# Expert tiles transposed by VectorE in 32x32 blocks instead of TensorE, with loads ahead and on two queues

## Chip, cores and metric

The kernel runs on one core of a Trainium2 chip. The metric is device time in microseconds (us). The kernel before takes 638.38 us, the median of 3 runs (637.48 to 639.96).

## What is computed

The reference is one block of a transformer: gated linear cross-attention with 16 heads of 32, then a mixture of 8 experts of which each token takes 2. There are 4 batches of 512 tokens, 1024 context rows each, and width 512, all in float32. Cut to what matters:

```python
x = x + xattn(layernorm(x), ctx, Wq, Wg, bg, Wkv, Wo)
xn = layernorm(x)
w, sel = top_k(xn @ Wr, 2)               # two experts for each token
gate = one_hot(sel) weighted by softmax(w)
for e in range(8):
    out = out + gate[..., e] * (xn @ We[e] + be[e])
x = x + out
```

## The kernel before

**Attention.** For each batch the kernel makes keys and values of the context in eight tiles, sums them to a small matrix per head, projects queries and gates, and adds the output projection to `x`. TensorE's instructions are kept in the order in which the program writes them (`matmul` at L85, `transpose` at L88). The other engines' instructions are ordered by a scheduler when the program is built, unless an edge or a `keep_in_program_order` pins them; each engine and each DMA queue then works in that fixed order and waits on semaphores.

**Routing.** `choose` normalizes a batch's tokens, makes the router's logits and takes the two largest. `dispatch` counts tokens per expert and lets GpSimd scatter each token's normalized row, with two numbers behind it (where the result goes, and the first choice), into `stream`, a DRAM buffer with one region for each expert. A row there has ROW = 514 elements, 2,056 bytes.

**Expert tiles.** `listed` makes, on the chip, a list of tiles of 128 consecutive stream rows: for each, the row at which it starts and its expert. `run` works through a list. In `rows(j)` SyncE reads the start from the list into a register (L624) and loads the 128 rows (L632) into `xg`, which lies in one of five buffers (three with tag `cT`, two with tag `v`). Four TensorE transposes (`transposed`, L220) turn `xg` into PSUM, and ScalarE copies the result to `xgT` (tag `qT`, four buffers, which the attention's queries use as well). `expert(j)` multiplies with the expert's weights in eight TensorE instructions, VectorE adds the bias into `y` (L659, three buffers), and GpSimd computes each row's home (`at`, L665) and scatters `y` to `result` in DRAM (L670).

There are two lists. The early one has 17 tiles (EARLY) that are full of tokens of the first three batches; four of them run ahead of the last batch's output projection, the others among its routing. The late one is made after the last `dispatch`; 18 tiles (SURE) always run, and up to four more stand in two nested branches (L835), which were not taken here. Before the late list, tiles of `empty` rows are written behind each expert's last token (fills, L775). Rows of the late list wait for all writes to the stream.

**The end.** `fetch(q)` loads the results of two output tiles back in two DMAs of 512 KB, `add(t)` adds both choices to `x` with two VectorE operations (L803), `store(t)` writes an output tile from ScalarE's queue. `at_step` says after which late tile each of these stands. The first eight output tiles' results are complete after the late tile of index DONE_2 - 1 (8 tiles), the next four's after DONE_3 (14 tiles), and the last four's after all.

**The inputs' loads.** SyncE's queue issues all loads, in program order where `load` (L92) is used, among them the experts' weights (one DMA of 1 MB per expert, during the second and third batch's attention).

Of the kernel before, what the change touches and what calls it, by code (L numbers as in the profile page):

```python
# [1 line left out]

# [7 lines left out]
F32 = mybir.dt.float32  # L10
# [5 lines left out]
ET = mybir.EngineType  # L16

P = 128
B, L, S, D = 4, 512, 1024, 512
E, F = 8, 512  # L20
HD = 32
NC = D // P
# [26 lines left out]
def xattn_moe_kernel(  # L49
# [39 lines left out]
        tc.keep_in_program_order(nc.tensor.transpose(dst, src, ident))  # L89


    def load(dst, src):  # L92
        tc.keep_in_program_order(nc.sync.dma_start(out=dst, in_=src))

    def load_ctx(b, s):
        t = cpool.tile([P, ROW], F32, tag="cT", name=f"cT_{b}_{s}")
# [15 lines left out]
    wo_sb = wpool.tile([P, NC, D], F32, tag="wo", name="wo_sb")  # L112
    wr_sb = wpool.tile([P, NC, E], F32, name="wr_sb")
    bg_sb = wpool.tile([P, NC], F32, name="bg_sb")
    we_sb = wpool.tile([P, E, NC, F], F32, name="we_sb")

    ctx_tiles = {}
    ctx_tiles[0, 0] = load_ctx(0, 0)
# [162 lines left out]
    def kv_tiles(b, lo, hi, between=None):  # L281
        for s in range(lo, hi):
            nxt = (b, s + 2) if s + 2 < NS else (b + 1, s + 2 - NS)
            if nxt[0] < B and nxt != (0, 2):
                ctx_tiles[nxt] = load_ctx(*nxt)
            if b in (1, 2) and s % 2 == 0:
                e = (b - 1) * E // 2 + s // 2
                load(we_sb[:, e], we[e])
            if (b, s) == (3, 0):
                load(stream[SLOTS : SLOTS + P, :], empty)  # L290
            if s == 0:
                sums[b] = pkv.tile([P, NC, 2 * P], F32, tag="kvs", name="kvs")
            k = made.pop(s) if s in made else keys(b, s)
            if (b, s) == (0, 0):
                made[1] = keys(0, 1)
            v = values(b, s)
            if s > 0:
                kv_add(sums[b], s - 1, *pending[b])
            pending[b] = k, v
            if between is not None:  # L300
                between(s - lo)
        if hi == NS:
            kv_add(sums[b], NS - 1, *pending[b])
# [314 lines left out]
    def run(lists, lo, n, early):  # L618
        why = "clamped to the tiles of the streams and to the experts where it is computed"
        no_i, row_i, ranked = lists  # L620

        def rows(j):

            row = nc.values_load(  # L624
                row_i[0:1, j : j + 1], [ET.SP], min_val=0, max_val=SLOTS,
                skip_runtime_bounds_check_because=why,
            )
            if j % 5 < 3:
                xg = cpool.tile([P, ROW], F32, tag="cT", name="xg")
            else:  # L630
                xg = kvpool.tile([P, ROW], F32, tag="v", name="xg", bufs=2)
            load = nc.sync.dma_start(out=xg, in_=stream[ds(row, P), :])  # L632
            if early:
                behind(load, written["stream"][: 2 * NT * (B - 1)], "tokens of the tile")
                early_loads.append(load)
                for put in scatters.get(B - 1, []):
                    tc.declare_no_dep(load.ins, put.ins, reason=full_already)
            else:
                behind(load, written["stream"], "tokens of the tile")
            xT = work.tile([P, NC, P], F32, tag="qT", name="xgT", bufs=NC)  # L640
            transposed(xT, xg)
            return xT, xg

        def expert(j, xT, xg):
            no = nc.values_load(
                no_i[0:1, j : j + 1], [ET.PE, ET.DVE], min_val=0, max_val=E - 1,
                skip_runtime_bounds_check_because=why,
            )
            pe = pmm.tile([P, F], F32, tag="mm", name="pe")
            for c in range(NC):  # L650
                matmul(
                    out=pe,
                    lhsT=xT[:, c, :],
                    rhs=we_sb[:, ds(no, 1), c, :].rearrange("p o f -> p (o f)"),
                    start=(c == 0),
                    stop=(c == NC - 1),
                )
            y = kvpool.tile([P, F], F32, tag="k", name="y")
            nc.vector.tensor_tensor(  # L659
                y, pe, be_sb[:, ds(no, 1), :].rearrange("p o f -> p (o f)"), ALU.add  # L660
            )
            home_i = small.tile([P, 1], U32, tag="to", name="to", bufs=8)

            at = small.tile([P, 1], F32, tag="at", name="at", bufs=8)
            nc.gpsimd.tensor_scalar(  # L665
                at, xg[:, D + 1 : D + 2], ranked[:, j : j + 1], xg[:, D : D + 1],
                ALU.is_equal, ALU.add,
            )
            nc.gpsimd.tensor_scalar(home_i, at, unread[:, j : j + 1], None, ALU.min)
            put = nc.gpsimd.indirect_dma_start(  # L670
                out=result,
                out_offset=bass.IndirectOffsetOnAxis(ap=home_i, axis=0),
                in_=y,
                in_offset=None,
            )
            apart(put, "result", "each choice has a row; rows without a token go unread")
            for got in read_back:
                tc.declare_no_dep(put.ins, got.ins, reason="no token of these is in the tile")

        ready = rows(lo)  # L680
        for j in range(lo, n):
            cur, ready = ready, rows(j + 1) if j + 1 < n else None
            expert(j, *cur)
            yield


# [5 lines left out]
    for b in range(B):  # L692
# [10 lines left out]
        if not more:  # L703
            whole = per_expert("whole")
            nc.vector.tensor_scalar(whole, counts[b - 1], float(1 - P), None, ALU.add)
            full = tiles_of(whole, "full")
            held = [tiles_of(counts[1], "held2"), tiles_of(counts[2], "held3")]
            none = per_expert("none")
            nc.vector.memset(none, 0.0)
            ahead = per_expert("ahead")  # L710
            nc.vector.tensor_tensor(ahead, held[0], full, ALU.min)
            early_groups = spans([none, ahead, full], "A")
            early_list = listed(early_groups, EARLY, "A")
            be_sb = wpool.tile([P, E, F], F32, tag="wkv", name="be_sb")
            load(
                be_sb.rearrange("p e f -> p (e f)"),
                be.rearrange("(o e) f -> o (e f)", o=1).to_broadcast([P, E * F]),
            )
            early = run(early_list, 0, EARLY, True)
        products(qTs, z, aT)  # L720
        if more:
            xs[b + 1] = load_x(b + 1)
# [46 lines left out]
    nc.vector.tensor_tensor(ends, counts[B - 1], region[:, 0, :], ALU.add)  # L769
    for e in range(E):  # L770
        row = nc.values_load(
            ends[0:1, e : e + 1], [ET.SP], min_val=0, max_val=SLOTS - P,
            skip_runtime_bounds_check_because="a region has room for all tokens",
        )
        fill = nc.sync.dma_start(out=stream[ds(row, P), :], in_=empty)  # L775
        apart(fill, "stream", "rows behind the last token of a stream")
        for load in early_loads:
            tc.declare_no_dep(fill.ins, load.ins, reason="behind all tokens of the stream")
# [3 lines left out]
    homes = [(wpool, "wq"), (wpool, "wg"), (wpool, "wo"), (big, "xT"), (big, "aT")]  # L782
    fetched = {}

    def fetch(q, tiles):

        pool, tag = homes[q % len(homes)]
        yt = pool.tile([P, 2, 2, F], F32, tag=tag, name=f"y_{q}")
        for u in range(2):
            load = nc.sync.dma_start(out=yt[:, u], in_=flat[:, 2 * q + u])  # L790
            tc.keep_in_program_order(load)
            behind(load, written["result"][: EARLY + tiles], "results of the tokens")
            for put in written["result"][EARLY + tiles :]:
                tc.declare_no_dep(load.ins, put.ins, reason="no token of these is in the tile")
            read_back.append(load)
            fetched[2 * q + u] = yt[:, u]
# [16 lines left out]
    at_step = {}  # L813
    first, last = 2 * NT, (B - 1) * NT
    for q in range(first // 2):
        at_step.setdefault(DONE_2 + 2 + q, []).append((fetch, q, DONE_2))
    for q in range(first // 2, last // 2):
        at_step.setdefault(DONE_3 + 2, []).append((fetch, q, DONE_3))
    for t in range(last):
        step = min(DONE_2 + 3 + t, SURE - 1 - (last - 5 - t) // 2)  # L820
        at_step.setdefault(step, []).append((add, t))
        at_step.setdefault(max(step + 1, DONE_2 + 5), []).append((store, t))

    def also(j):
        for what, *of in at_step.pop(j, []):
            what(*of)

    for j, _ in enumerate(run(late_list, 0, SURE, False)):
        also(j)

    many = nc.values_load(
# [1 line left out]
        skip_runtime_bounds_check_because="the streams hold no more tiles",  # L833
    )
    with tc.If(many > SURE):  # L835
        for _ in run(late_list, SURE, SURE + 1, False):
            pass
        with tc.If(many > SURE + 1):
            for _ in run(late_list, SURE + 1, LATE, False):
                pass  # L840
    for j in sorted(at_step):
        also(j)
    for q in range(last // 2, TOK // P // 2):
        fetch(q, LATE)
    for t in range(last, TOK // P):
        add(t)
        store(t)
# [43 lines left out]
```

## Time and profile before

| what | value |
|---|---|
| median of 3 runs | 638.38 us |
| profiled execution: time | 640.01 us |
| profiled execution: span, first to last instruction | 638.3 us |
| mean granted TensorE clock | 0.984 |
| TensorE busy | 606.4 us, 95% of the span |
| VectorE, ScalarE, GpSimd busy | 37%, 21%, 17% |
| DMA traffic | 70.50 MB, mean 110 GB/s |
| expert tiles run | 17 early, 18 late |
| last product of an expert tile ends | 615.2 us |

A profile is one execution on the chip. PE is TensorE's matrix products and transposes, PEld its weight loads, DVE VectorE, ACT ScalarE, POOL GpSimd, SP SyncE; a q behind an engine's name means its instruction queue, which issues DMAs and waits. A group's line gives source line, engine, operation, out<-in, shape and count, then busy us, mean ns of one, and the idle time of the engine just before with what ended it. `pt` is the PSUM tile of a transpose, `pe` that of an expert tile's product, `pp` that of the counting matmuls in `dispatch`.

### The profile page before, as it was taken

The numbers are of one execution on the slowest core, as the hardware profiler recorded it, in microseconds if no ns is written. First come the engines' busy times: TensorE is split into PE (matmuls) and PEld (weight loads), VectorE is DVE, ScalarE is ACT, GpSimd is POOL, SyncE is SP. The second block draws the span as 40 slices with busy tenths as digits, with TensorE's granted clock in tenths as the row PEclk, the third lists the DMA queues.
The fourth block names the chain that finished last, engine by engine and source line by source line (L and its number), as shares of the span: only waits on it lengthen the run. The fifth ranks groups of instructions, "written<-read, shape, count | busy, mean of one in ns | idle before, by whom it ended". The sixth has DMA issues, their size and how long they took to land. (4 is left out here: it accounts for less than half of the span.)

```text
span 638.3 us, 6238 instructions
## 1 busy us (share of the span) xinstructions
PE 606.4 (95%) x2044; PEld 301.6 (47%) x2044; DVE 236.1 (37%) x562; ACT 135.5 (21%) x215; POOL 109.0 (17%) x244
## 2 busy tenths in 40 slices
PE   7999999999999999999999999999999999999950
PEld 3555543544564345455543544654444654444420
DVE  2222243126224521632534135148424272111583
ACT  1322222113322122042221113322111221111100
POOL 3100000000004000000230000005241354643420
PEclk9999999999999999999999999999999999999985
DMA  8611400220253023022130100033430269647768
GB/s 301 194 34 37 144 0 2 104 93 17 82 166 115 18 62 111 26 91 93 47 117 17 34 16 16 1 131 134 116 116 33 84 203 264 193 133 258 278 236 300
DMA packets 27376, 70.50 MB, mean 110 GB/s; under 512 B 4240, under 2 KB 4240, under 8 KB 25936
## 3 DMA queue, kind: packets, MB, share of 16 engines
q1 hardware_dynamic: 19680, 48.31, 23.7%
q0 software_dynamic: 5360, 17.60, 7.6%
q10 hardware_dynamic: 2304, 4.20, 1.8%
q8 instruction: 17, 0.28, 0.2%
q14 instruction: 15, 0.12, 0.1%
HBM read 45.93 MB, written 24.16 MB: 110 GB/s over the span
## 5 line engine op out<-in xcount | busy, mean ns | idle before, releaser
L86 PE MATMUL pe<-we_sb,xgT 128*128 x280 | 125.9, 594 | 1.1 <-issue 0.6
L86 PE MATMUL pk<-wkv_sb,cT 128*128 128x512 f32 x256 | 118.6, 608 | 4.6 <-DMA wkv_sb<-in_wkv_dram 4.6
L86 PE MATMUL pv<-wkv_sb,cT 128*128 128x512 f32 x256 | 114.9, 592 | 0.0
L86 PEld LDWEIGHTS pv<-wkv_sb,cT 128*128 128x128 f32 x256 | 48.6, 190 | 61.2 <-issue 61.0
L200 DVE TENSOR_SCALAR ex<-pk 128x512 f32<-128x512 f32 x32 | 22.0, 689 | 148.0 <-PE pk L86 148.0
L86 PEld LDWEIGHTS pe<-we_sb,xgT 128*128 128x128 f32 x280 | 50.6, 190 | 53.0 <-issue 52.0
L86 PEld LDWEIGHTS pk<-wkv_sb,cT 128*128 128x128 f32 x256 | 47.7, 194 | 58.1 <-issue 54.3
L257 POOL MEMSET v<- 128x4 f32 x32 | 3.3, 106 | 347.1 <-PE kvs L86 284.1
L201 ACT ACTIVATE ex<-ex 128x512 f32<-128x512 f32 x48 | 30.2, 630 | 138.7 <-DVE ex L200 128.8
L86 PE MATMUL pg<-xT,wg_sb 128*128 128x512 f32 x128 | 56.7, 595 | 0.0
L86 PE MATMUL pq<-xT,wq_sb 128*128 128x512 f32 x128 | 56.6, 596 | 0.0
L659 DVE TENSOR_TENSOR y<-pe,be_sb 128x512 f32<-128x512 f32 x35 | 24.1, 690 | 87.4 <-PE pe L86 73.5
L86 PE MATMUL po<-wo_sb,aT 128*128 128x512 f32 x128 | 55.6, 592 | 0.0
L225 ACT COPY xgT<-pt 128x512 f32<-128x512 f32 x35 | 20.3, 587 | 121.9 <-PE pt L89 103.5
L670 POOL DMA_INDIRECT result<-y,to x35 | 37.5, 1071 | 39.0 <-DVE y L659 32.1
L505 POOL DMA_INDIRECT stream<-row,slot x32 | 32.1, 1003 | 49.6 <-DVE cmp L533 22.5
L86 PEld LDWEIGHTS kvs<-v,k 128*128 128x128 f32 x256 | 33.3, 191 | 13.4 <-issue 13.4
L86 PEld LDWEIGHTS pg<-xT,wg_sb 128*128 128x128 f32 x128 | 24.0, 190 | 32.1 <-issue 32.1
L86 PEld LDWEIGHTS po<-wo_sb,aT 128*128 128x128 f32 x128 | 24.1, 190 | 29.2 <-issue 28.9
L86 PEld LDWEIGHTS pq<-xT,wq_sb 128*128 128x128 f32 x128 | 23.8, 190 | 27.3 <-issue 27.3
L86 PE MATMUL kvs<-v,k 128*128 128x129 f32 x256 | 34.0, 275 | 0.0
L202 DVE SCALAR_TENSOR_TENSOR k<-pk,ex 128x512 f32<-128x512 f32 x32 | 22.1, 691 | 24.1 <-ACT ex L201 24.0
(151 smaller groups left out, 445.6 us busy)
## 6 DMA issues: line engine op xcount, KB each, us to landing
xg<-stream SPq DMA_DIRECT2D x35, 257.0 KB
cT<-in_cT_dram SPq DMA_DIRECT2D x32, 256.0 KB
we_sb<-in_we_dram SPq DMA_DIRECT2D x8, 1024.0 KB
y<-result SPq DMA_DIRECT2D x16, 512.0 KB
x<-in_x_dram SPq DMA_DIRECT2D x16, 256.0 KB
out_dram<-x ACTq DMA_DIRECT2D x16, 256.0 KB
stream<-empty SPq DMA_DIRECT2D x9, 257.0 KB
wkv_sb<-in_wkv_dram SPq DMA_DIRECT2D x8, 256.0 KB
```

Source lines behind the costliest of these rows:

```text
L86: tc.keep_in_program_order(nc.tensor.matmul(**operands))
L200: nc.vector.tensor_scalar(ex, src, 0.0, None, ALU.min)
L201: nc.scalar.activation(ex, ex, AF.Exp)
L202: nc.vector.scalar_tensor_tensor(dst, src, 0.0, ex, ALU.max, ALU.add)
L225: nc.scalar.copy(dst, pt)
L257: nc.gpsimd.memset(v[:, :, P : P + 1], 1.0)
L505: put = nc.gpsimd.indirect_dma_start(out=stream, out_offset=bass.IndirectOffsetOnAxis(ap=slots[i][:, t, :], axis=0), in_=rows[t], in_offse ...
L659: nc.vector.tensor_tensor(y, pe, be_sb[:, ds(no, 1), :].rearrange("p o f -> p (o f)"), ALU.add)
L670: put = nc.gpsimd.indirect_dma_start(out=result, out_offset=bass.IndirectOffsetOnAxis(ap=home_i, axis=0), in_=y, in_offset=None,)
```

## The change

Rows of an expert tile are loaded in an arrangement in which each 32x32 block needs only to be transposed in place, which VectorE does in one instruction from `xg` to `xgT`. The 32 partitions of group i hold columns 128i to 128i + 127 of all 128 rows: four loads of 32 partitions each, in pieces of 512 bytes, and a fifth load of 8 bytes a row for the two numbers behind the row (`of`). The expert weights are loaded in the matching order of rows, four DMAs for each expert instead of one. The first call of `run` issues five tiles' loads and three transposes; from then on, step j issues the loads of tile j + 5, the transpose of tile j + 3 and the products of tile j, with `y` kept behind that transpose on VectorE. The early list's first call stands ahead of the attention's last products. Fills and all but the last four output tiles' result loads go to ScalarE's queue; additions and stores of output tiles that stood at the last late step or behind it (t of 6 to 11) stand behind the branches.

```diff
     def load(dst, src):
-        tc.keep_in_program_order(nc.sync.dma_start(out=dst, in_=src))
+        latest["load"] = nc.sync.dma_start(out=dst, in_=src)
+        tc.keep_in_program_order(latest["load"])
...
+    we_rows = we.rearrange("e (c f) i n -> e i f c n", f=HD)
...
-                load(we_sb[:, e], we[e])
+                for i in range(NC):
+                    load(we_sb[ts(i, HD), e], we_rows[e, i])
...
-            load = nc.sync.dma_start(out=xg, in_=stream[ds(row, P), :])
-            if early:
...
+            of = small.tile([P, 2], F32, tag="of", name="of", bufs=8)
+            rows_of = stream[ds(row, P), :]
+            parts = []
+            for i in range(NC):
+                parts.append(
+                    (
+                        xg[ts(i, HD), 0:D].rearrange("t (j f) -> t j f", j=NC),
+                        rows_of[:, ts(i, P)].rearrange("(j t) f -> t j f", t=HD),
+                    )
+                )
+            parts.append((of, rows_of[:, D:ROW]))
+            for dst, src in parts:
+                load = nc.sync.dma_start(out=dst, in_=src)
+                latest["load"] = load
...
+            return xg, of
+
+        def turned(xg, of):
             xT = work.tile([P, NC, P], F32, tag="qT", name="xgT", bufs=NC)
-            transposed(xT, xg)
-            return xT, xg
-
-        def expert(j, xT, xg):
+            latest["turn"] = nc.vector.transpose(
+                xT.rearrange("p c (j t) -> p j c t", t=HD),
+                xg[:, 0:D].rearrange("p (j c f) -> p j c f", j=NC, f=HD),
+            )
+            return xT, of
+
+        def expert(j, xT, of):
...
-                at, xg[:, D + 1 : D + 2], ranked[:, j : j + 1], xg[:, D : D + 1],
+                at, of[:, 1:2], ranked[:, j : j + 1], of[:, 0:1],
...
-        ready = rows(lo)
+        loaded, ready = [], []
+
+        def ahead(j):
+            if j + 5 < n:
+                with tc.issue_after(latest["load"].ins) if latest else nullcontext():
+                    loaded.append(rows(j + 5))
+            if j + 3 >= lo and loaded:
+                ready.append(turned(*loaded.pop(0)))
+
+        for j in range(lo - 5, lo):
+            ahead(j)
+        yield
         for j in range(lo, n):
-            cur, ready = ready, rows(j + 1) if j + 1 < n else None
-            expert(j, *cur)
+            ahead(j)
+            with tc.issue_after(latest["turn"].ins):
+                expert(j, *ready.pop(0))
             yield
...
             early = run(early_list, 0, EARLY, True)
+            next(early)
         products(qTs, z, aT)
...
-            ends[0:1, e : e + 1], [ET.SP], min_val=0, max_val=SLOTS - P,
+            ends[0:1, e : e + 1], [ET.Activation], min_val=0, max_val=SLOTS - P,
...
-        fill = nc.sync.dma_start(out=stream[ds(row, P), :], in_=empty)
+        fill = nc.scalar.dma_start(out=stream[ds(row, P), :], in_=empty)
...
-    def fetch(q, tiles):
+    def fetch(q, tiles, queue):
...
-            load = nc.sync.dma_start(out=yt[:, u], in_=flat[:, 2 * q + u])
+            load = queue.dma_start(out=yt[:, u], in_=flat[:, 2 * q + u])
...
-        at_step.setdefault(DONE_2 + 2 + q, []).append((fetch, q, DONE_2))
+        at_step.setdefault(DONE_2 + 2 + q, []).append((fetch, q, DONE_2, nc.scalar))
     for q in range(first // 2, last // 2):
-        at_step.setdefault(DONE_3 + 2, []).append((fetch, q, DONE_3))
+        at_step.setdefault(DONE_3 + 2, []).append((fetch, q, DONE_3, nc.scalar))
     for t in range(last):
-        step = min(DONE_2 + 3 + t, SURE - 1 - (last - 5 - t) // 2)
+
+        step = DONE_2 + 3 + t if DONE_2 + 3 + t < SURE - 1 else SURE
         at_step.setdefault(step, []).append((add, t))
-        at_step.setdefault(max(step + 1, DONE_2 + 5), []).append((store, t))
+        at_step.setdefault(max(step + 1, DONE_2 + 5) if step < SURE else SURE, []).append((store, t))
...
-    for j, _ in enumerate(run(late_list, 0, SURE, False)):
+    late = run(late_list, 0, SURE, False)
+    next(late)
+    for j, _ in enumerate(late):
         also(j)
...
     for q in range(last // 2, TOK // P // 2):
-        fetch(q, LATE)
+        fetch(q, LATE, nc.sync)
```

## The prediction

> **What bounds the kernel now.** I read the page's busy shares and clock first, then the chain of work that ended last, the groups, the waits of SyncE's queue, and stage windows for the end.
>
> ```profile
> PE 606.4 (95%) x2044; PEld 301.6 (47%) x2044; DVE 236.1 (37%) x562; ACT 135.5 (21%) x215; POOL 109.0 (17%) x244
> ...
> PEclk9999999999999999999999999999999999999985
> DMA  8611400220253023022130100033430269647768
> ```
>
> TensorE is busy 95% of the span at full granted clock, until the last slices. So work taken off TensorE counts in full, unless a wait takes its place. The chain (start, length, what) shows how one expert tile stands on it:
>
> ```profile
> 457.62 0.60 PE pt L89 x4
> ...
> 458.24 0.59 ACT xgT L225
> ...
> 458.88 3.70 PE pe L86 x8
> 462.58 0.44 PE pt L89 x4
> ...
> 549.78 0.44 PE pt L89 x4
> 550.22 3.44 PE pe L86 x8
> ...
> 605.60 8.51 DMA y<-result
> ...
> 620.28 2.92 DMA result<-y,to
> ...
> 628.13 5.44 DMA y<-result
> ```
>
> An expert tile is 0.44 us of transposes (pt) and 3.44 us of products (pe), back to back, 3.87 us in all. From 604 us the chain leaves TensorE for result loads. The groups give the prices of what moves:
>
> ```profile
> L659 DVE TENSOR_TENSOR y<-pe,be_sb 128x512 f32<-128x512 f32 x35 | 24.1, 690 | 87.4 <-PE pe L86 73.5 <-DMA result<-y,to 9.3 <-remote 4.6
> L803 DVE SCALAR_TENSOR_TENSOR x<-y,gates,x 128x512 f32<-128x512 f32 x32 | 23.6, 752 | 10.0 <-DMA y<-result 7.3 <-SPq L835 2.2
> L89 PE MATMUL pt<-ident,xg 128*128 128x128 f32 x140 | 20.9, 274 | 0.0
> ```
>
> The timeline has TensorE with two tiles' products and no transposes between them (next fence, first line): 7.03 us for 16, so products alone keep the 3.44 us pace. The SyncE line after it, from the same view, has three row loads issued at a spacing of 0.86 us.
>
> ```profile
> 537.88 7.03 PE L86 MATMUL pe<-we_sb,xgT 128*128 x16
> ```
> ```profile
> 450.03 2.06 SPq L632 DMA_DIRECT2D xg<-stream  x3
> ```
>
> The windows of the end (us, then PE, PEld, DVE, ACT, POOL, clock, DMA share, GB/s):
>
> ```profile
> 580.00:604.00 24.00, 24.00 (x76) 11.78 (x75) 8.45 (x12) 3.52 (x6) 9.87 (x14) 1.00 0.81 306
> 604.00:620.00 16.00, 11.17 (x32) 5.03 (x30) 12.78 (x19) 1.17 (x2) 3.65 (x3) 0.93 0.66 231
> 620.00:638.30 18.30, 0.00 (x0) 0.00 (x0) 8.39 (x12) 0.00 (x0) 0.96 (x1) 0.50 0.79 283
> ```
>
> The last product ends at 615.2 (16 from 608.14 in 7.03). A tail of 23.1 us follows: VectorE's additions, result loads and stores.
>
> **The change, part by part.** *Removed:* 35 tiles x 0.437 = 15.3 us of transposes on TensorE, and 35 ScalarE copies (0.59 each) that were hidden.
>
> *VectorE transpose.* Not in the trace. All 128x512 operations on VectorE take between 0.54 (the normalisation, xn) and 3.35 us (the reciprocal of L341). I take 0.69, the price of y and of most rows in this shape; both ends are kept. At 0.69 VectorE has 0.69 + 0.69 + 1.53 (two additions) = 2.9 us in its fullest tile step, under 3.44: hidden. At 3.35 it has 4.04 in a plain tile, and is the bound.
>
> *Five loads where there was one.* SyncE issues a tile's load in 0.86 us, 0.31 of that the register load, which stays single. Four more cost 0.51 each by the eight result loads at 580.94 (4.10 us for 8), at most 0.65 by the small bias loads at 11.64 (4.38 for 7, each also waiting for an earlier one). So 2.9 to 3.5 us a tile; I take 3.1: just under 3.44, hidden. Cover: SyncE now waits 79.4 us in 20 waits at L632 for buffers that the PE transposes held; a buffer is now free once VectorE has read it. In packets, the trace has 85 ns for 2,056 bytes, 13 ns for 128 and 9 ns for 4, so by that slope I estimate 28 ns for 512 bytes: 32 x 28 + 8 x 9 = 1.0 us a tile on each DMA engine instead of 0.7, in 3.44. Landing took 2.7 to 2.9 us (issue at 537.92, GpSimd's `at` released at 540.78; 450.03 and 452.96), and 450.03 to 453.55 had five such loads under way together.
> The Trainium skill (DMA: Bandwidth & Descriptors, Rules for kernel authors) speaks against this part: coalesce small transfers, since under 64 KB they are mostly overhead, and splitting by partitions brings nothing. Were the fixed cost of about 2 us that the page gives (Anatomy of one DMA) serial, five would be 10 us a tile, and the late list alone 18 x (10 - 3.87) = 110 us longer; the overlapping loads above contradict a serial reading, and the sum does not use it.
>
> *Expert weights* in four loads each: 24 more issues x 0.5 = 12 us on SyncE during the attention stages, where it waits 348.2 us for products of TensorE (L93); no cost. Without that cover a context load comes 1.5 us later, two tiles ahead of its use.
>
> *Where the early list starts.* Products of tile 0 began at 458.88. Now: rows land near 455 (450.0 + 3 x 0.55 + 2.9), the attention products end at 457.6, VectorE is busy with `aT` until 459.5. If the transpose goes between these, 457.6; behind them, 460.2. I take 459.3.
>
> *Between the lists.* From the first product to the counting matmuls of the last dispatch (516.77) lie 9 transposes, 3.9 us: these come at 513.3, 3.5 earlier. The late rows wait for all stream writes and start then at 537.92 - 3.5 = 534.4 (the eight fills go from SyncE to ScalarE, idle there; the scatters end last, so this gains nothing). Fourth load issued 1.65 later, landed 2.7 after that, transposed 0.7: products at 539.5. TensorE is through with the early list at 513.3 + 0.6 + 7 x 3.44 = 538.0. So 1.5 us of new stall, where before PE ran almost through. Queued around this transpose on VectorE are the y of the last early tiles, which wait for scattered results to leave their buffers (before: 5.30 us at 538.46 and 3.98 at 546.18, released by the result scatter). If the transposes stand behind these, products start near 546; I take 1.4 us for it, nearer to the low end, since GpSimd's first late `at` (540.78) did stand ahead of an early tile's scatter (541.93) before. So 540.9.
>
> *Late list.* 18 x 3.44 = 61.9: last product at 602.8, against 615.2. y of tile j stands behind the transpose of j+3 on VectorE; it waits only if rows are three tiles late, and six PSUM tiles cover it.
>
> *The tail.* Before, the y of the last three tiles stood behind additions that waited for y loads: they ran at 610.69, 616.25 and 618.84, though two had their products earlier. Now six output tiles are added and stored only behind the branches, so the last y follows its product. Then VectorE alone: 602.8 + 0.7 (y) + 0.6 (branch) + 12 x 0.765 (six tiles) + 8 x 0.765 (the last four) = 619.4. The last loads fit beside it: last scatter issued at 604, landed 2.9 later, four loads of 512 KB that took 5.4 to 8.5 us before: in at 613 to 616, needed from 613. From the last addition's end at 635.14 to the span's end were 3.1 us: 622.5. The result loads on ScalarE's queue cost nothing there, as no copies are left behind them; row loads no longer stand behind them (SyncE held its last three from 577.8 to 585.9).
>
> **Sum.** The profiled execution took 640.01 us with a span of 638.3, 1.6 over the median of 638.38. Span 622.5 is 15.8 less; 638.38 - 15.8 = 622.6.
>
> **The rivals.** *Stalls eat part of it* (0.22): late products from 546 (+5.1), start 460.2 (+0.9), loads in the tail at 8.5 (+3): to 631.6. For it: y's waits above. Against: the transposes are free to go first.
>
> *VectorE becomes the bound* (0.06): a transpose near the reciprocal's 3.35. Twelve late tiles at 4.04 and six at 5.57 are 81.9 instead of 61.9: 642.6 less the early tiles' cover of some 2, about 640. Against: nothing else in this shape comes near 3.35.
>
> *Row loads land too slowly* (0.16), the case on the slower side: in the trace the hardware queues' DMAs signal eight semaphores in turn, and each issue waits for the DMA eight before it. Five a tile then make a tile cost 5/8 of the landing time. It binds TensorE from 5.5 us landing, and eats the whole gain at 4.3 us a tile, 6.9 us landing. For it: rows issued at 585.92 behind result loads reached GpSimd at 596.86. Against: 2.7 to 2.9 elsewhere, and the last rows may be issued before result loads begin. At 8 us through the late list: 18 x (5.0 - 3.44) = 28, so 651.
>
> *The change doesn't do what it says* (under 0.01): y is tied behind the transpose three tiles on, so the lead holds.
>
> **How the numbers follow.** Forecast 0.55, partial 0.22, VectorE 0.06, slow landing 0.16, rest 0.01. Half a percent, 3.2 us, is about what measurement tells from none. Faster: 0.55 + 0.22 = 0.77; same 0.06 (VectorE's case); slower 0.17. Low end: start 457.6 (-1.7), no order loss (-1.4), transposes at 0.54, and the runs' own -0.9: 618. I say 617. High end: the partial case's 631.6 with SyncE at 3.5 a tile (+1) and part of the way to VectorE's case: 635.
>
> **What would show it.** No pt on xg in the groups; one DVE transpose group x35 near 0.69 us. The chain in the late list with pe 3.44 after pe 3.44 and no wait; late products from 539 to 546; the last near 603; y right behind it; VectorE's additions in one run to the end. Wrong: `pe` waiting for DVE xgT in the middle of a list, SyncE issuing without a pause and TensorE idle each tile, row loads landing after more than 5.5 us, or additions waiting for y loads in the tail.

## The result, and the profile after

The changed kernel takes 640.85 us, the median of 20 runs (638.39 to 642.08); the kernel before took 638.55 beside it (637.27 to 640.95). The ratio is 1.0029, interval 1.0017 to 1.0040: slower by 0.3%, where 622.6 was forecast. The profiled execution took 640.36 us with a span of 638.7. That of the kernel before took 640.01, 1.6 over its median, so the two traces show 0.4 us of the 2.3 between the medians.

The page first: busy time, granted clock and DMA share, then the groups of the changed kernel and its DMA issues.

```profile
PE 594.0 (93%) x1904; PEld 288.6 (45%) x1904; DVE 258.2 (40%) x597; ACT 115.2 (18%) x180; POOL 109.4 (17%) x244
...
PEclk9999999999999999999999999999999999999585
DMA  8611500430353014124120100033354376568786
...
L666 DVE STREAM_TRANSPOSE xgT<-xg 128x512 f32<-128x512 f32 x35 | 24.8, 708 | 33.0 <-DMA xg<-stream 33.0
...
xg<-stream SPq DMA_DIRECT2D x140, 64.0 KB, 2.2
...
y<-result ACTq DMA_DIRECT2D x12, 512.0 KB, 6.2
```

TensorE has 12.4 us less to do, the transpose costs 0.708 us on VectorE, and a row load lands in 2.2 us. Up to there the prediction holds. The timeline of TensorE (start, length, what, idle time before it and its releaser) shows the trouble:

```profile
511.96 76.16 PE L86 MATMUL pe<-we_sb,xgT 128*128 x176
601.72 13.48 PE L86 MATMUL pe<-we_sb,xgT 128*128 x24 [13.61 <-DVE xgT L666]
```

Twenty-two tiles run without a pause from the last dispatch to 588.1, with no stall between the lists. Then TensorE waits 13.61 us for the transpose of late tile 15. The last product ends at 615.2, where it ended before. The reason stands in VectorE's timeline:

```profile
581.60 0.71 DVE L666 STREAM_TRANSPOSE xgT<-xg 128x512 f32<-128x512 f32 x1 [3.22 <-DMA xg<-stream]
596.18 1.54 DVE L846 SCALAR_TENSOR_TENSOR x<-y,gates,x 128x512 f32<-128x512 f32 x2 [13.87 <-DMA y<-result]
598.25 1.54 DVE L846 SCALAR_TENSOR_TENSOR x<-y,gates,x 128x512 f32<-128x512 f32 x2 [0.53 <-DMA y<-result]
599.70 0.68 DVE L687 TENSOR_TENSOR y<-pe,be_sb 128x512 f32<-128x512 f32 x1
...
600.96 0.71 DVE L666 STREAM_TRANSPOSE xgT<-xg 128x512 f32<-128x512 f32 x1
```

The two additions at 596.18 belong to output tile 6, those at 598.25 to tile 7. The change writes them behind the branches. In the order in which VectorE works they stand ahead of y of late tile 11 and of the last three transposes, and they wait for the last two of eight result loads, which were issued at 588.68 and 591.51 and had landed at 596.16 and 598.22. The rows of late tile 15 had been there since 587.23, before TensorE ran out of work. As this order shows, the pin on an addition holds it behind the instruction of its engine written before it in the same block of code only. Behind the branches begins a new block, its first addition has nothing to stand behind, and the scheduler moved it forward.

The windows of the end, in the columns shown before:

```profile
580.00:604.00 24.00, 10.39 (x22) 4.41 (x21) 7.93 (x12) 0.00 (x0) 8.11 (x12) 0.72 0.88 281
604.00:620.00 16.00, 11.20 (x22) 4.39 (x20) 12.32 (x20) 0.00 (x0) 5.26 (x5) 0.82 0.79 284
620.00:639.00 19.00, 0.00 (x0) 0.00 (x0) 9.09 (x13) 0.00 (x0) 0.96 (x1) 0.50 0.67 246
```

While TensorE stands still from 588 to 602, the DMA engines are busy: 0.88 from 580 to 604. The tail behind the last product is 23.5 us, 23.1 before.

### The profile page after: what moved, and what is told of

The parts are those of the page before. It is cut to its first block, busy times and chain, and to the rows that moved or that the text cites. A ratio compares the mean times of both kernels' runs of the same rounds, so it can differ in the third digit from the quotient of the medians.

```text
span 638.7 us, 6416 instructions
## 1 busy us (share of the span) xinstructions
PE 594.0 (93%) x1904; PEld 288.6 (45%) x1904; DVE 258.2 (40%) x597; ACT 115.2 (18%) x180; POOL 109.4 (17%) x244
## 5 line engine op out<-in xcount | busy, mean ns | idle before, releaser
L86 PE MATMUL pe<-we_sb,xgT 128*128 x280 | 125.0, 606 | 13.7 <-DVE xgT L666 13.6
L86 PEld LDWEIGHTS pe<-we_sb,xgT 128*128 128x128 f32 x280 | 53.7, 194 | 81.7 <-issue 63.6
L666 DVE STREAM_TRANSPOSE xgT<-xg 128x512 f32<-128x512 f32 x35 | 24.8, 708 | 33.0 <-DMA xg<-stream 33.0
L846 DVE SCALAR_TENSOR_TENSOR x<-y,gates,x 128x512 f32<-128x512 f32 x32 | 23.4, 747 | 24.3 <-DMA y<-result 23.9
```

Source lines behind the costliest of these rows:

```text
L86: tc.keep_in_program_order(nc.tensor.matmul(**operands))
L666: latest["turn"] = nc.vector.transpose(xT.rearrange("p c (j t) -> p j c t", t=HD), xg[:, 0:D].rearrange("p (j c f) -> p j c f", j=NC, f=HD),)
L846: nc.vector.scalar_tensor_tensor(xt, yt[:, 1 - i, :], gates[:, t, i : i + 1], xt, ALU.mult, ALU.add)
```

## The experiments

Theory A was that the moved additions alone lose the gain; rival B, that the last tiles' rows land late beside result loads. Later came C, that GpSimd's scatters fall behind, and D, that what is transferred at the end binds, not TensorE. In each step the kernel before ran beside, at medians of 638.03 to 638.57 us. This table holds all runs, in us. The first three columns come from each kernel's trace, of one run that lies within 1.8 us of the median; the time is the median, and the ratio is to the kernel before:

| kernel | last product | last scatter issued | last four loads from | time | ratio, interval |
|---|---|---|---|---|---|
| before | 615.2 | 620.3 | 623.4 | 638.4 | |
| after | 615.2 | 621.1 | 625.5 | 640.85 | 1.0029 (1.0017 to 1.0040) |
| undo_steps | 607.9 | 616.5 | 621.3 | 640.20 | 1.0038 (1.0018 to 1.0057) |
| adds_pinned | 607.3 | 611.1 | 620.0 | 637.58 | 0.9995 (0.9977 to 1.0013) |
| after_ordered | 609.5 | 611.4 | 620.8 | 637.51 | 0.9983 (0.9966 to 0.9999) |
| both | 599.3 | 608.0 | 616.3 | 636.54 | 0.9969 (0.9956 to 0.9983) |
| pool_alone | 614.0 | 620.9 | 625.4 | 641.16 | 1.0039 (1.0020 to 1.0059) |
| pool_adds | 605.6 | 611.3 | 617.0 | 634.69 | 0.9948 (0.9928 to 0.9968) |
| pool_both | 598.7 | 605.6 | 615.2 | 635.11 | 0.9954 (0.9937 to 0.9970) |
| pool_spread | 600.1 | 608.1 | 616.0 | 635.66 | 0.9957 (0.9940 to 0.9974) |
| lead2 | 606.9 | 609.5 | 616.6 | 635.51 | 0.9956 (0.9939 to 0.9972) |
| lead2_y4 | 608.3 | 611.0 | 618.6 | 637.00 | 0.9970 (0.9953 to 0.9986) |
| pool_both_ordered | 598.4 | 605.0 | 614.8 | 633.46 | 0.9916 (0.9887 to 0.9945) |
| spread_sp | 599.5 | 605.8 | 614.2 | 630.65 | 0.9869 (0.9840 to 0.9899) |
| before_pinned | 613.5 | 615.0 | 618.1 | 634.87 | 0.9941 (0.9924 to 0.9957) |
| before_ordered | 613.8 | 615.3 | 618.4 | 635.02 | 0.9942 (0.9922 to 0.9963) |
| before_spread | 613.9 | 615.4 | 618.5 | 637.61 | 0.9982 (0.9967 to 0.9998) |
| before_light | 614.1 | 617.1 | 620.3 | 635.53 | 0.9953 (0.9935 to 0.9971) |
| both_light | 598.8 | 604.8 | 611.5 | 631.39 | 0.9885 (0.9860 to 0.9910) |
| spread_sp_light | 599.2 | 605.6 | 608.8 | 625.23 | 0.9786 (0.9768 to 0.9804) |

**The additions' place.** Four kernels, the last of them a control on the kernel before.

```diff
-        step = DONE_2 + 3 + t if DONE_2 + 3 + t < SURE - 1 else SURE
+        step = min(DONE_2 + 3 + t, SURE - 1)                               # adds_pinned
+        step = min(DONE_2 + 3 + t, SURE - 1 - (last - 5 - t) // 2)         # undo_steps
# stores in these and in both, as in the kernel before: max(step + 1, DONE_2 + 5)
# both: min(DONE_2 + 5 + t, SURE - 1), and the result loads behind the last rows:
-        at_step.setdefault(DONE_2 + 2 + q, []).append((fetch, q, DONE_2, nc.scalar))
+        at_step.setdefault(SURE - 6, []).append((fetch, q, DONE_2, nc.sync))
-        at_step.setdefault(DONE_3 + 2, []).append((fetch, q, DONE_3, nc.scalar))
+        at_step.setdefault(DONE_3 + 2, []).append((fetch, q, DONE_3, nc.sync))
# before_pinned, in the kernel before:
-        step = min(DONE_2 + 3 + t, SURE - 1 - (last - 5 - t) // 2)
+        step = min(DONE_2 + 3 + t, SURE - 1)
```

> The changed kernel, with the additions of output tiles 6 to 11 at the last late step instead of behind the branches, so that VectorE does them behind the last transposes and behind y of the last late tile. Theory A (the additions that were put behind the branches float ahead of the last three transposes and make VectorE wait for result loads): TensorE's wait of 13.6 us for xgT shrinks to under 5 us, the last product ends near 599 to 604 instead of 615.2, the time is 622 to 628. Rival B (the last tiles' rows land late behind result loads, whatever VectorE does): TensorE still waits 10 us or more ahead of the last three tiles, now for the rows' DMA, the last product ends past 610, the time is 635 to 641.

> The changed kernel with the steps of the additions and stores as in the kernel before; transposes, loads and queues stay changed. Theory A: as with the pinned additions TensorE no longer waits over 5 us ahead of the last three tiles and the last product ends near 599 to 604, but the first addition behind the branches still stands ahead of the last y on VectorE, as before, so the tail stays near the 23 us of the kernel before: 624 to 631. Rival B: TensorE waits 10 us or more for rows, 635 to 641.

> Additions at the last late step, and the result loads of the first twelve output tiles issued by SyncE behind the last row loads instead of by ScalarE among them. Theory A with a small part of B (row loads of the last three tiles landed in 5.6 to 7.3 us beside result loads, instead of 2.2): no wait of TensorE over 1 us in the late list, last product near 598 to 600, row loads land in about 2.2 us to the end, time 618 to 624. Rival B: the same last product, and all of the gain over the pinned additions alone, which would stay near 640. If neither is the cause: last product past 610.

> A control: the kernel before, with nothing but the additions of output tiles 6 to 11 at the last late step, so that none of them stands ahead of the last y. The transposes stay on TensorE. Theory A says that a part of what pinned additions bring is not the transposes' own: the last product ends at 615 as before, the last y follows it within 1 to 2 us instead of 3.6, and the tail shortens by 2 to 6 us: 632 to 637. If the tail is set by result loads and not by the additions' order, the time stays within 2 us of before.

TensorE's longest wait fell from 13.61 us to 6.19 (adds_pinned), 5.78 (undo_steps) and 0.79 (both), and its last product came earlier by 7.3 to 15.9 us. For the first two theory A had asked for more, under 5 us and a last product at 599 to 604; in adds_pinned the y at 596.09, which stands ahead of the next transpose on VectorE, waits 7.28 us for a scatter. The times did not follow at all: those of adds_pinned and undo_steps lie where rival B had them, though TensorE does not. undo_steps finished its products 7.3 us earlier than the changed kernel and took as long. both has TensorE's whole gain, in one run of the late list,

```profile
537.19 62.07 PE L86 MATMUL pe<-we_sb,xgT 128*128 x144 [0.79 <-DVE xgT L666]
```

and is 1.5 us below the kernel before; it missed its 618 to 624 by 12.5. The control gains 3.2 us with no transpose moved. So theory A is right about the larger part of TensorE's stall and wrong about the time: something behind TensorE holds the end. Comparing both with the kernel before, piece by piece from the last product on: to the last scatter's issue 8.75 us instead of 5.1, from there to the last loads 8.3 instead of 3.1, to the first of them landed 4.8 and 4.7, from there to the last addition's end 10.3 instead of 7.0, and 3.4 instead of 3.2 to the end. That is 12.4 of 15.9 us given back; the two spans are 3.5 us apart. The windows of both (DMA share and GB/s are the last two columns) and SyncE's waits from 595 on:

```profile
596.00:604.00 8.00, 3.26 (x8) 1.14 (x6) 4.96 (x8) 0.00 (x0) 2.43 (x2) 1.00 1.03 413
604.00:612.00 8.00, 0.00 (x0) 0.00 (x0) 6.12 (x9) 0.00 (x0) 2.17 (x2) 0.52 1.03 411
```
```profile
SPq L881 <- SPq L881: 10.6, 4, 6.2
```

The transfer engines are full. Scatters issued at 590.51 to 593.16 landed 8.3 to 8.8 us later, where most before them took 2.8 to 3.3. The last four y have three buffers: the first of them waits until 598.94 for a scatter's landing, the last until 606.57. At the branches SyncE waits until every DMA on the hardware queues has landed (steps of it are released at 611.66, 614.21 and 615.61, each as an output store lands, the first 6.97 us after its issue), and only then issues the last loads.

**GpSimd's order (theory C).** In the changed kernel the scatter of a tile comes 9 to 12 us behind its product (late tiles 0 to 8; tile 3: product 550.35, scatter 562.26), in the kernel before mostly 1 us. GpSimd's own timelines, the kernel before first:

```profile
570.15 1.07 POOL L670 DMA_INDIRECT result<-y,to  x1 [0.76 <-DVE y L659]
```
```profile
570.46 0.39 POOL L693 TENSOR_SCALAR at<-of,rankedB 128x1 f32<-128x1 f32 x1 [1.23 <-DMA of<-stream]
570.94 0.29 POOL L697 TENSOR_SCALAR to<-at,unread 128x1 uint32<-128x1 f32 x1
571.38 1.08 POOL L698 DMA_INDIRECT result<-y,to  x1 [0.15 <-issue]
```

Before, a scatter waits for its y. Now `at` of tile 11 stands ahead of the scatter of tile 6 and waits for tile 11's rows. The eighth late tile's scatter, behind which result loads start, is issued at 574.60 instead of 577.89, although its product is 12.8 us earlier (564.09 and 576.88).

```diff
+            keep = (lambda i: i) if early else tc.keep_in_program_order
-            nc.gpsimd.tensor_scalar(at, ...)       # and home_i, and the scatter put
+            keep(nc.gpsimd.tensor_scalar(at, ...))
# pool_adds, pool_both: the same in adds_pinned and both; pool_spread: pool_both with
+    for h, step in enumerate((9, 10, 11, 12, 13, 13, 14, 14)):
+        queue = nc.scalar if step <= 12 else nc.sync
+        at_step.setdefault(step, []).append((fetch, h // 2, DONE_2, queue, (h % 2,)))
```

> The changed kernel with one thing more: the late tiles' GpSimd instructions keep the order of the program, at, to and scatter of one tile before those of the next. Theory C (GpSimd's at of a tile five ahead stands in front of a scatter and waits for that tile's rows, so that in the changed kernel every scatter comes 10 to 13 us behind its products, and the result loads start no earlier than before): the scatter of the eighth late tile is issued near 566 instead of 574.6, the first result load near 569 instead of 577.6, scatters 1 to 3 us behind their products; the additions that float ahead still hold VectorE, but for loads that come some 8 us earlier, so TensorE's wait falls from 13.6 to about 5 us and the time to 628 to 634. Theory A alone: within 3 us of the changed kernel's 640.9. A bound by the bytes at the end: the last product earlier by 5 us or more, and the time all the same over 636.

> GpSimd's order and the additions' (the last late step) both pinned, result loads from ScalarE's queue among the row loads as in the changed kernel. Theory C: result loads from near 569, TensorE's wait ahead of the last tiles under 4 us, last product 599 to 603, last scatter issued by 605 instead of 608 to 621, time 622 to 628. If the 411 GB/s that the transfers reach at the end is the bound whatever the order: 634 or more.

> GpSimd's order and the additions' pinned, the twelve output tiles' result loads from SyncE behind the last row loads (588 to 593). Theory C: scatters keep up, so the last y follows its product, last scatter near 601 to 603 instead of 608.0; but the result loads start as late as without the pinned scatters, so the gain is only that: 628 to 633. Bound by bytes from 588 on (14 MB at 411 GB/s are 34 us): 627 or more.

> As the one before, with the eight result loads of the first eight output tiles one by one: at late steps 9 to 12 from ScalarE's queue, then from SyncE's, which has issued its last row load by then. Theory C with bytes spread: TensorE's wait in the late list under 2 us, last product 599 to 601, result loads from near 569, time 620 to 626. If starting the loads early is worth nothing, the same as with the loads behind: 628 to 633.

C is a small part: pinned scatters are worth 2.9 us (adds_pinned to pool_adds) and 1.4 (both to pool_both), and nothing alone. None of the four came to the time that C gave, and pool_spread's 635.66 misses both of its ranges. The pins moved the eighth scatter only to 570.5 to 571.1, since y itself came 4 to 6 us behind its product: it stands behind the transpose of j + 3, and that waits for the rows of j + 3. The first result load, where it was not placed later, came at 576.2 to 576.9. In pool_alone the scatter had landed at 573.7, and ScalarE waited on until 576.13 for a row load of SyncE's queue that signals the same semaphore.

**The transposes' lead, and a fourth buffer.** Both with the additions and GpSimd's order pinned.

```diff
-            if j + 3 >= lo and loaded:
+            if j + (3 if early else 2) >= lo and loaded:
+    for h, step in enumerate((7, 8, 9, 10, 11, 12, 12, 13)):       # scalar up to step 12
# lead2_y4: y and k with bufs=4
```

> GpSimd's order and the additions pinned, and in the late list the transposes two tiles ahead of the products instead of three, so that y of a tile stands behind the transpose of j + 2, whose rows are there; result loads one by one from late step 7. Pinning GpSimd alone left y 4 to 6 us behind its product, waiting behind the transpose of j + 3, and the result loads at 576. Expected: y within 2 us of its product from late tile 5 on, the scatter of the eighth late tile issued near 567, the first result load near 570 instead of 576 to 577. Theory D: those 6 us come off the end, 627 to 631. If starting the transfers earlier is worth nothing: 634 to 636, as the pinned kernels.

> The same with a fourth buffer for y, so that a y waits for the scatter four tiles back. In the pinned kernels y waited for scatters that land 5 to 8 us after issue beside result loads. If that wait sets the last scatter (605 to 611): 1 to 3 us below lead2; if the transfers' bytes do: the same as lead2 within 1 us.

The loads did start earlier (572.90) and gained nothing. ScalarE issued six in 3 us, the four row loads of late tile 13 took from 572.86 to 578.47 to be issued, and TensorE waited 5.92 us again. With the fourth buffer the time is 1.5 us longer, which neither of its theories had; why is open.

**The bytes (theory D).** Half of the result loads left out, in three kernels:

```diff
-            load = queue.dma_start(out=yt[:, u], in_=flat[:, 2 * q + u])
+            load = queue.dma_start(out=yt[:, u, 0:1], in_=flat[:, 2 * q + u, 0:1])
-                    xt, yt[:, 1 - i, :], gates[:, t, i : i + 1], xt, ALU.mult, ALU.add
+                    xt, yt[:, 0, :], gates[:, t, i : i + 1], xt, ALU.mult, ALU.add
```

> The kernel before, with half of the result loads left out: of a token's two results only the first is read back, and added twice. 4.2 MB less, 10.2 us at the 411 GB/s of the end. Theory D (the end is set by the transfers that begin with the first result load, in both kernels, and not by TensorE's last product): TensorE's last product stays at 615, and what follows it shortens by 4 to 8 us: 630 to 634. If not the transfers but the order of additions sets the end: within 2 us of before.

> The kernel with the additions pinned and the result loads behind the rows, with the same half of the result loads left out. Theory D: with light transfers the 15.9 us that TensorE is earlier come through for the most part: 621 to 627, 6 to 11 us below the kernel before with the same half left out, where the full kernels differ by 1.5. If the tail is a chain of latencies that bytes don't set: 631 to 635, and the difference between the two stays near 1.5.

> The fastest kernel so far (630.65 us, last product 599.5), with the same half of the result loads left out as in before_light (635.53 us, last product 614.1). Theory D: with light transfers the 14.6 us between the last products come through for the most part, 10 us or more between the two times: 621 to 626. If a chain of latencies behind the last scatter holds it whatever the bytes are: 628 to 631.

The cut takes 2.8 us off the kernel before, between its two theories, 5.1 off both and 5.4 off spread_sp (below). The kernel before and both are then 4.1 us apart instead of 1.5, less than the 6 to 11 of theory D, and both_light's time lies in the other theory's range; the kernel before and spread_sp are 10.3 apart instead of 7.4, as D had it. So the bytes hold the kernels with an early last product back more than the kernel before, but they are a part of what holds them: half of the result loads would be 10.2 us at 411 GB/s. The windows of spread_sp, then of spread_sp_light:

```profile
600.00:612.00 12.00, 0.00 (x0) 0.00 (x0) 6.95 (x11) 0.00 (x0) 3.29 (x5) 0.66 0.95 378
```
```profile
600.00:612.00 12.00, 0.00 (x0) 0.00 (x0) 11.06 (x17) 0.00 (x0) 5.71 (x7) 0.68 0.83 279
```

With the same products done, VectorE works 11.06 us of these twelve instead of 6.95: the additions wait less for loads.

**Additions in one order across the branches.** In both, output tile 12's first addition, which waits for the last loads, stood ahead of those of tiles 8 to 11, whose loads had landed; the same rule of the pin let it.

```diff
+            for name in before_add:          # after_ordered: also the y traced last
+                tc.add_manual_dep(one.ins, name, <issue order only>)
+            before_add[:] = [one.ins.name]
# pool_both_ordered, from pool_both; before_ordered the same with DONE_2 + 3:
-        step = min(DONE_2 + 5 + t, SURE - 1)
+        step = min(DONE_2 + 5 + t, SURE - 1) if t < first else SURE
# spread_sp: this, GpSimd pinned, lead of 2, and on SyncE's queue alone
+    for h, step in enumerate((8, 9, 10, 11, 12, 12, 12, 12)):
+        at_step.setdefault(step, []).append((fetch, h // 2, DONE_2, nc.sync, (h % 2,)))
# before_spread: the additions' order in the kernel before, rows pinned, loads at steps 10 to 16
```

> The changed kernel with one thing more: the additions are kept in one order across the branches, and each behind y of the last late tile traced before it, which is what the prediction took for granted. Loads, queues and GpSimd's order as changed. Theory A (the additions alone): no wait of TensorE over 2 us, last product 599 to 602, time 622 to 628. Theory D (the transfers and the chain behind the last scatter set the end): TensorE waits 3 to 7 us for late scatters and rows, last product 600 to 606, and the time is 632 to 636, only 5 to 9 below the changed kernel.

> The kernel with GpSimd's order and additions pinned and the result loads behind the rows (635.1 us), with the additions in one order across the branches, so that none of output tiles 8 to 11 stands behind the first of output tile 12, which waits for the last result loads. There 15 additions ran between the landing of the last loads and the end, 10.3 us; 8 have to. Expected by the count: 7 x 0.67 = 4.7 us less of that run, part of it back where the last load lands later than the additions need it: 630.5 to 633. If the end is the loads' landing alone: 634 to 636.

> The control: the kernel before, transposes on TensorE, with the additions in the same one order. Three of the eleven additions behind its last load go ahead of it. Expected: 632 to 635, up to 2 us below the kernel before with additions at the last late step (634.9). What the transposes on VectorE are worth with both ends in order is then the difference from pool_both_ordered: 1 to 4 us.

> Everything in order (GpSimd, additions across the branches), transposes two tiles ahead in the late list, and the result loads one by one on SyncE's queue between the last row loads (late steps 8 to 11, the rest at 12), so that no burst of 3 MB stands ahead of rows and scatters as in lead2. Theory D: TensorE waits under 2 us, last product 599 to 602, the transfers start near 575 instead of 588 and keep the engines busy; last scatter issued by 606, time 626 to 631. If the row loads can't share with result loads at all: TensorE waits over 5 us, 633 to 637.

> The last control: the kernel before, transposes on TensorE, with everything that made spread_sp fast as far as it applies: additions in one order across the branches, SyncE's row loads kept in program order, and the result loads between and behind the last ones instead of eight in a burst. Its GpSimd scatters already follow their products by 1 us. If the order of loads and additions alone makes 630.65 us: 630 to 632. If the transposes on VectorE are the rest: 633.5 to 635.5, near the ordered kernel before (635.0), and the transposes are worth 3 to 5 us.

after_ordered is the change with the one thing that the prediction took for granted, and nothing else: 637.5, so that premise is worth 3.3 us, not 18, and less even than theory D's 632 to 636 said. TensorE still waits 2.64 and 4.69 us:

```profile
589.84 5.40 PE L86 MATMUL pe<-we_sb,xgT 128*128 x8 [2.64 <-DVE xgT L667]
599.92 9.58 PE L86 MATMUL pe<-we_sb,xgT 128*128 x16 [4.69 <-DVE xgT L667]
```

Order at the end is worth 1.7 us (pool_both to pool_both_ordered, just over its range), and nothing in the kernel before (634.87 to 635.02). The chains of waits of both and of pool_both_ordered show it:

```profile
616.34 4.79 DMA y<-result
621.13 0.02 issue
621.15 8.05 DVE x L846 x12
```
```profile
616.17 9.26 DMA y<-result
625.43 0.02 issue
625.46 0.76 DVE x L849
626.22 0.03 issue
626.24 0.75 DVE x L849
```

Fifteen additions behind the first of the last loads, twelve of them in one run, became two behind the last of them; the end then stands on that load's landing, 9.26 us after issue beside the output stores. spread_sp is the fastest, 630.65. It puts one result load between two tiles' rows; TensorE runs the late list in 62.07 us. Its place was forecast (626 to 631). before_spread missed both of its theories: loads spread in this way with the transposes on TensorE are slower than before_ordered, with 637.6. Its additions begin at 599.51 instead of 591.69, and its chain ends with twenty of them in a run on VectorE, sixteen in before_ordered. The best kernel with transposes on TensorE is before_pinned at 634.87, so from best to best moving them is worth 4.2 us of the 15.3 that TensorE saves. It depends on what stands around them: 1.6 us from before_ordered to pool_both_ordered, 7.0 from before_spread to spread_sp.

## Why the prediction was wrong

- *Transposes removed, 15.3 us*: right. PE's busy time fell by 12.4, because the 24 products behind the stall took 13.48 us, where 24 in the run ahead of it take 10.4 (176 in 76.16); in both, which has no such stall, it fell by 15.5 (590.9).
- *VectorE's transpose, 0.69*: right, 0.708. Rival VectorE-bound: no.
- *Five loads, 3.1 us a tile; landing 2.7*: right, 3.0 to 3.2 in most tiles and 2.2. The Trainium skill (DMA: Bandwidth & Descriptors, Rules for kernel authors), weighed against this part, advises not to split. Of the 110 us of a serial reading the 176 products without a pause show none; the 2 us behind them are, on that page, of DMAs that GpSimd issues, and SyncE issues these.
- *First product 459.3; late products 540.9 with 1.5 + 1.4 us of stall*: earlier, at 457.4, and the late list followed the early one with no stall. Better than forecast by 1.9 and 2.9 us.
- *y behind the transpose of j + 3 "waits only if rows are three tiles late, and six PSUM tiles cover it"*: rows were that late, y came 3 to 6 us behind its product (late tiles 0 to 10), and PSUM did cover it for TensorE. The step priced y for TensorE alone. Behind y stand the scatter and the result loads, and these had no cover.
- *"Now six output tiles are added and stored only behind the branches, so the last y follows its product"*: this step failed. Place in the program was taken for place on VectorE, though the profile of before already had y of the last three tiles behind additions. Cost: TensorE's 13.61 us, and 3.3 us of the time when put right (after_ordered).
- *"The last loads fit beside it"*, in at 613 to 616, needed from 613: this step failed too, and it is the larger one. In both, with the last product at 599.3, the last loads were issued at 616.3; in the fastest kernel that loads all results, at 614.2. The sum set the end as TensorE's last product plus VectorE's work, a tail of 19.7 us (602.8 to 622.5); with the additions in order (after_ordered) the tail is 26.3, behind a last product 6.7 us later than forecast, and in both it is 35.5. 8.4 MB of result loads, 4.2 MB of stores and the last scatters stand at the end as well, from 588 on in both, and 12.6 MB take 30.7 us at the 411 GB/s of both. The half of these loads was worth 5.1 us there; how the rest of the tail divides is open (below).
- *"The result loads on ScalarE's queue cost nothing there"*: wrong. The first row load of late tile 15, issued at 579.30 beside them, landed 7.12 us later, and SyncE issued the next tile's first load, which signals the same semaphore, only then (586.55, after 586.42). The Trainium skill (the same page, Rules for kernel authors) says that spreading DMAs over issuing engines brings no bandwidth, since all run on the same sixteen DMA engines. No run here moves only the queue, but the fastest kernel has the result loads back on SyncE's.
- *Rival, rows landing too slowly (651)*: its mechanism came, but only for the last three tiles, and for less.

Not settled: of the 15.6 us by which spread_sp's last product is earlier, 7.4 come through, and 10.3 of 14.9 with half the loads. What takes the rest then, the stores, the scatters' landing or the wait at the branches, was not tried apart.

## What to carry to other kernels

Before work taken off the busiest engine is counted, follow its results to the end of the program: when the last transfers start, how many bytes are left, and what they take at the rate that the trace shows. Work saved ahead of a full transfer stage buys only what that stage can start earlier. An instruction written later is not queued later: read the order on each engine, and look at what stands ahead of the instructions that feed the critical one, on GpSimd too.

## What was not expected of the hardware

The changed kernel in windows of 8 us, in the columns shown before:

```profile
580.00:588.00 8.00, 8.00 (x19) 3.23 (x17) 0.71 (x1) 0.00 (x0) 1.07 (x4) 1.00 1.00 327
588.00:596.00 8.00, 0.12 (x1) 0.00 (x0) 0.00 (x0) 0.00 (x0) 1.34 (x2) 0.66 1.01 305
596.00:604.00 8.00, 2.28 (x3) 1.18 (x4) 7.22 (x11) 0.00 (x0) 5.69 (x7) 0.50 0.62 211
```

An idle stretch costs more than itself: after 13.6 us of waiting TensorE's granted clock was 0.50 (596 to 604 us), and the next 24 products took 3.1 us longer. A short one does it too: behind the 2.64 us in after_ordered eight products took 5.40 us, where they take 3.6 at the full clock. The Trainium skill (TensorE: Matmul & The Clock Gate, What's actually happening) states such a half clock after an idle window, and the row agrees. And a full DMA share is not one rate. With row loads in 512-byte pieces under way the changed kernel's engines moved 327 GB/s at a share of 1.00 and 305 at 1.01 (580 to 596 us); with result loads, stores and scatters alone those of both moved 413 and 411 at 1.03. The 512-byte packets were about an eighth of the bytes; an estimate from the median packet times (27 ns, and 159 for 4,096 bytes) gives 395 GB/s for such a mix. The 4,096-byte packets took longer beside them, 183 and 206 ns in the mean of these windows against 161 in both; what slows them is not shown.
